# Shared-expert down products two chunks behind gate and up, with a third pair of operand buffers

## The chip, the cores and the metric

The kernel runs on one core of a Trainium2 chip. The metric is device time in microseconds, one launch, for the whole computation. Lower is better. The kernel before takes 1871.48 us, the median of 3 runs (1870.2 to 1871.99).

## The reference

A token stream of 2 x 2048 tokens with 256 features goes through three residual stages: half of a mixture-of-experts feed-forward, attention in groups of 64 tokens, and half of the same feed-forward again, each on a layer norm of the stream. Cut to what matters here:

```
x = x + 0.5 * ffn(layernorm(x))          # T = 4096 tokens, H = 256
x = x + attn(layernorm(x))               # 16 heads of 16, causal, groups of 64
x = x + 0.5 * ffn(layernorm(x))

ffn(x):  xn = rmsnorm(x);  probs = softmax(xn @ router_w.T);  top 2 of E = 8
         each expert takes its first 640 tokens:
           eout = (silu(xg @ rg[e]) * (xg @ ru[e])) @ rd[e]         # 256 -> 1024 -> 256
           routed += weight * eout
         shared = (silu(x @ sg) * (x @ su)) @ sd                    # 256 -> 2048 -> 256, all tokens
         return shared + routed
```

Everything is float32 at the interface.

## The kernel before

Every float32 operand of a large product is held as two float16 planes, a high and a low part. A product is then three float16 matmuls (high x high, high x low, low x high; the list TERMS).

The program has four phases. Phase a: layer norm and routing of 32 token tiles for the first feed-forward, beside the shared expert of 5 of the 8 token blocks (a block is 512 tokens). Phase b: the 8 experts of the first feed-forward. Phase c: the shared expert of the remaining 3 blocks, attention for 32 token tiles with layer norm and routing for the second feed-forward, and the shared expert of all 8 blocks of it. Phase d: the 8 experts of the second feed-forward.

The shared expert (`shared`) goes over the 2048 hidden features in 16 chunks of 128. For one chunk of one block, `gate_up` makes two groups of six matmuls of 512 columns (L306), the gate group and the up group, each into a tile "pgu" of PSUM; there are three such tiles in the pool `ps_gu`. Then the activation is made in the tile "sl" (float32): ScalarE applies Silu (L317, phase a) or Tanh (L313, phase c), in phase c VectorE completes it with L314, and VectorE multiplies in the up group (L319). ScalarE rounds the product to float16 into "hh" (L321), and VectorE writes the remainder into "hl" (L322). The pair hh and hl comes from the pool `hp` with two buffers; "sl" has two of its own.

The down products (`down`, L330) multiply hh and hl of a chunk with the chunk's rows of sd: twelve matmuls of 256 columns that add up over the 16 chunks in two PSUM tiles "po". After the last chunk VectorE adds the residual "xr" (L363, two instructions), and SP's queue stores the two halves of the block (L366). The tiles xr have two buffers in all, one block's worth, and are loaded by `res_load` (L344) ahead of chunk 2 of the block.

The down products of a chunk are not traced right after its gate and up products. `defer` holds one function back:

```
    def defer(self, f):
        p, self.pend = self.pend, f
        if p is not None:
            p()
```

So in the order of the source TensorE gets gate and up of chunk c, down of chunk c-1, gate and up of chunk c+1, and so on. The end of a phase calls `defer(None)` for the last one. The experts (`experts`, phases b and d) use the same `gate_up`, `down` and `defer`, with 640 tokens per expert in 8 chunks.

Beside the shared expert runs the work of the token tiles, written as generators: `tile1` (phase a) and `tile2` with `attn_tile` (phase c). `drive` takes one slot of this side work for every three steps of the shared expert, which is one slot per chunk. A tile of attention goes through the transposes L174, L533, L564 and L590 (DMAs on SP's queue), the projections L603 (tiles pqk, pv, pao), the scores L541 (psc), the products with the values L572 (py), and many small operations of VectorE, ScalarE and GpSimd; where it waits for a DMA it lets two slots pass. Its PSUM tiles come from the pool `ps_m` (three buffers in phases a and c).

The source gives a priority, not a fixed order: a planner with a timeline of its own orders the instructions of every engine, and an instruction whose operands are late in that timeline can be passed by later ones. [...]

Of the kernel before, what the change touches and what calls it, by code (L numbers as in the profile page):

```python
# [8 lines left out]
F32 = mybir.dt.float32  # L9
# [6 lines left out]
ALU = mybir.AluOpType  # L16
# [4 lines left out]
P = 128  # L21
H = 256
# [3 lines left out]
WS = 16.0  # L26
XP = UP * WS
NB = 8
BT = 512
# [8 lines left out]
class Net:  # L38
    def __init__(self, ctx, tc):
        self.tc = tc  # L40
        self.nc = nc = tc.nc
        pool = lambda name, bufs, **k: ctx.enter_context(tc.tile_pool(name=name, bufs=bufs, **k))
        self.cst = pool("cst", 1)
        self.wsh = pool("wsh", 1)
        self.tok = pool("tok", YB)
        self.xb = pool("xb", NB)
        self.xe = pool("xe", 2)
        self.sm = pool("sm", 2)
        self.dr = pool("dr", 1, space=DRAM)
        self.ps_gu = pool("ps_gu", 3, space=PSUM)  # L50
        self.pend = None
        self.anchor = None
        c = self.cst
        self.tri = c.tile([P, P], BF16, name="tri")
        nc.gpsimd.memset(self.tri, 1.0)
        nc.gpsimd.affine_select(
            out=self.tri, in_=self.tri, pattern=[[1, P]], compare_op=ALU.is_gt,
            fill=0.0, base=0, channel_multiplier=-1)
        self.ones = c.tile([P, P], BF16, name="ones")
        nc.gpsimd.memset(self.ones, 1.0)  # L60
        self.iota8 = c.tile([P, E], F32, name="iota8")
        for e in range(E):
            nc.gpsimd.memset(self.iota8[:, e:e + 1], float(e))
        self.mhalf = c.tile([P, 8], F32, name="mhalf")
        nc.gpsimd.memset(self.mhalf, -0.5)
        self.e1 = c.tile([P, 4], F32, name="e1")
        nc.gpsimd.memset(self.e1, 2.718281828459045)
        tk = self.sm.tile([P, 32], I32, name="tk", bufs=1)
        nc.gpsimd.iota(tk, pattern=[[P, 32]], base=0, channel_multiplier=1)
        self.tokid = c.tile([P, 32], F32, name="tokid")  # L70
        nc.vector.tensor_copy(self.tokid, tk)

    def phase(self, name, ntok, nout, nx=1, nsl=2):
        ctx = ExitStack()
        tc = self.tc
        pool = lambda n, bufs, **k: ctx.enter_context(
            tc.tile_pool(name=f"{name}_{n}", bufs=bufs, reuse_waits="tile", **k))
        self.ntok = ntok
        self.nsl = nsl
        self.hp = pool("hp", 2)  # L80
        self.xs = pool("xs", nx)
        self.raw = pool("raw", 2)
        self.at = pool("at", 1)
        self.ps_out = pool("po", nout, space=PSUM)
        self.ps_m = pool("pm", 5 - nout, space=PSUM)
        ctx.callback(lambda: self.defer(None))
        return ctx

    def m1(self, shape, dt, name):
        return self.ps_m.tile(shape, dt, name=name, tag="m")  # L90

    def defer(self, f):
        p, self.pend = self.pend, f
        if p is not None:
            p()

    def split(self, hi, lo, src):

# [249 lines left out]

    def shared(self, b, xb, src, dst, tanh=False, res=None):
        nc = self.nc  # L350
        outs = [self.ps_out.tile([P, BT], F32, name="po", tag="po") for _ in range(2)]
        for c in range(16):
            if c == 2 and res is None:
                res = self.res_load(src, b)
            h = self.hbuf()
            yield from self.gate_up(self.sgu[:, c], xb, h, tanh)

            def fin(c=c, h=h):
                self.down(outs, 4, h, self.sdw[:, :, c], c, 16)
                if c < 15:  # L360
                    return
                for i in range(2):
                    nc.vector.scalar_tensor_tensor(  # L363
                        out=res[i], in0=outs[i].rearrange("p (t f) -> p t f", f=H), scalar=0.5 / WS,
                        in1=res[i], op0=ALU.mult, op1=ALU.add)
                    nc.sync.dma_start(  # L366
                        out=dst[b * BT + i * 2 * P:b * BT + (i + 1) * 2 * P].rearrange("(t p) f -> p t f", p=P),
                        in_=res[i])

            self.defer(fin)  # L370
            yield
# [299 lines left out]
def run_slots(tiles, until):  # L671
    while not until():
        for _ in tiles.steps():
            pass


def drive(main, tiles, rate):

    credit = 0.0
    side = iter(())  # L680
    for _ in main:
        credit += 1.0
        for _ in range(2):
            if next(side, "end") == "end":
                break
        if credit >= rate:
            for _ in side:
                pass
            credit -= rate
            if not tiles.done():  # L690
                side = tiles.steps()
    for _ in side:
        pass


@with_exitstack
def macaron(ctx, tc, x, w_qkv, ln_w, w_proj, router_w, rg, ru, rd, sg, su, sd, out):
    nc = tc.nc
    x = x.rearrange("b s h -> (b s) h")
    out = out.rearrange("b s h -> (b s) h")  # L700
    n = Net(ctx, tc)
    R1 = n.route_init(0)
    R2 = n.route_init(1)
    R2["acc"] = out
    x2 = n.dr.tile([T, H], F32, name="x2")
    fbs = {}
    used = set()

    def new_fb(h, b):
        def get(t):  # L710
            if t == 0:
                assert h == 1 or (1, b) in used
                fb = fbs[(h, b)] = n.front_new()
                fb["pe"] = h == 1 and b < PEB
            return fbs[(h, b)]
        return get

    def tail(R, h, b, t):
        if t == 3:
            yield from n.route(R, b, fbs[(h, b)])  # L720

    def tile1(j):
        b, t = divmod(j, 4)
        y = n.load_tile(x, b, t)
        yield
        yield
        yield from n.front_steps(y, t, new_fb(1, b))
        yield from tail(R1, 1, b, t)

    def tile2(j):  # L730
        b, t = divmod(j, 4)
        yield from n.attn_tile(R1, j, x2, new_fb(2, b))
        yield from tail(R2, 2, b, t)

    def ready(h, b):
        return lambda: (h, b) in fbs and fbs[(h, b)]["n"] == 4

    def all_shared(key, b, src, dst, **k):
        yield from n.shared(b, fbs[key]["xb"], src, dst, **k)
        used.add(key)  # L740

    def fill(R):

        for e in range(E):
            z = n.raw.tile([P, 5, XW], F32, name="zero")
            nc.gpsimd.memset(z, 0.0)
            nc.vector.tensor_scalar_add(z[:, :, H], n.tokid[:, 0:5], float(T + e * CAP))
            nc.sync.dma_start(out=R["xg"][e * CAP:(e + 1) * CAP].rearrange("(t p) f -> p t f", p=P), in_=z)
            yield

    with n.phase("a", BT, 2, 10):
        n.ident = n.at.tile([P, P], F32, name="ident")
        make_identity(nc, n.ident)
        n.load_router(router_w)
        tiles = Tiles(tile1, 32, GAP_A)
        run_slots(tiles, ready(1, 0))
        n.load_shared(sg, su, sd)
        for _ in fill(R1):
            pass
        for b in range(NA):  # L760
            run_slots(tiles, ready(1, b))
            if b == 2:
                tiles.extra.append(fill(R2))
                for i in range(NA, NB):
                    nc.sync.dma_start(out=R1["acc"][i * BT:(i + 1) * BT], in_=x[i * BT:(i + 1) * BT])
            drive(all_shared((1, b), b, x, R1["acc"]), tiles, RATE_A)
        run_slots(tiles, tiles.done)
        cur = {}
        for _ in n.expert_load(R1, 0, cur):
            pass  # L770
    with n.phase("b", CAP, 3):
        n.experts(R1, rg, ru, rd, cur)
    with n.phase("c", BT, 2, 6, SLC):
        n.attn_init(w_qkv, ln_w, w_proj)
        tiles = Tiles(tile2, 32, GAP_C)
        for b in range(NA, NB):
            drive(all_shared((1, b), b, R1["acc"], R1["acc"], tanh=True), tiles, RATE_C)
        for b in range(8):
            run_slots(tiles, ready(2, b))
            drive(all_shared((2, b), b, x2, R2["acc"], tanh=True), tiles, RATE_C)  # L780
        run_slots(tiles, tiles.done)
        cur = {}
        for _ in n.expert_load(R2, 0, cur):
            pass
    with n.phase("d", CAP, 3):
        n.experts(R2, rg, ru, rd, cur)
# [10 lines left out]
SLC = 2  # L797
# [28 lines left out]
```

## Time and profile before

| | |
|---|---|
| median of 3 runs | 1871.48 us |
| the profiled execution's own time | 1875.79 us |
| its span, first to last instruction | 1874.1 us |
| mean granted TensorE clock | 0.994 |
| TensorE busy (matmuls) | 1786.8 us, 95% |
| VectorE busy | 1262.5 us, 67% |
| ScalarE busy | 942.1 us, 50% |
| GpSimd busy | 724.5 us, 39% |

Busy time counts the instructions of an engine as the profile draws them; matmuls are pipelined, so a drawn matmul is longer than the distance to the next one. PE stands for TensorE's matmuls, PEld for its weight loads, DVE for VectorE, ACT for ScalarE, POOL for GpSimd, SP for the queue that issues most DMAs. A row such as "L330 PE MATMUL po<-sdw,hl ... x1024 | busy, mean ns | idle" gives the line, the engine, what is written from what, the count, and the idle time of the engine just before such instructions with what ended it. In the view of waits a row is "engine line <- releaser: us in total, times, longest". By stage, phase a with the start takes about 0 to 340 us, phase b to about 690 us, phase c to about 1475 us, and phase d the rest; the phases overlap at their edges.

### The profile page before, as it was taken

To read this page: it belongs to the slowest core of one execution; us is meant where nothing else is said; L and a number is where in the kernel's file an instruction comes from. 1 tells how busy PE (TensorE), PEld (TensorE's weight loads), DVE (VectorE), ACT (ScalarE), POOL (GpSimd) and SP (SyncE) were. 2 spreads that over 40 slices of the span, in tenths; PEclk is the share of its full clock that TensorE was granted. 3 is DMA by queue.
4 is the path that set the end of the run, shared out by engine and by line. 5 is a ranking of instruction groups with operands and counts; after the bars stand their busy time and mean duration, and the time that the engine had idled before them with its cause. 6 is when DMAs were issued, how large, how long until landed. Compare 5 with 4: busy or idle time off the path is not lost.

```text
span 1874.1 us, 37396 instructions
## 1 busy us (share of the span) xinstructions
PE 1786.8 (95%) x13546; PEld 1191.7 (64%) x13546; DVE 1262.5 (67%) x3190; ACT 942.1 (50%) x1991; POOL 724.5 (39%) x943
## 2 busy tenths in 40 slices
PE   6899999999999999999999999999999999999996
PEld 3455555677777765666565655656566567777775
DVE  8756554456666656788888888888886556565663
ACT  5323323355555535666566666656643335555553
POOL 5743332011112223455757667575753001111122
PEclk9999999999999999999999999999999999999998
DMA  9742113045455424556657576766631304544542
GB/s 278 220 125 75 35 29 86 21 102 115 112 113 125 104 55 86 110 105 120 139 114 141 102 141 119 135 121 119 129 62 37 86 12 102 114 113 105 117 109 50
DMA packets 447481, 196.07 MB, mean 105 GB/s; under 512 B 302353, under 2 KB 444365, under 8 KB 447248
## 3 DMA queue, kind: packets, MB, share of 16 engines
q1 hardware_dynamic: 429632, 172.51, 41.1%
q0 software_dynamic: 17664, 21.17, 6.6%
q8 instruction: 106, 1.74, 0.4%
q14 instruction: 79, 0.65, 0.1%
HBM read 80.52 MB, written 52.33 MB: 71 GB/s over the span
## 4 chain that ended last, share of the span: by engine, by line
PE 57%; DVE 12%; POOL 10%; issue 9%; DMA 6%; ACT 4%; SPq 2%; POOLq 0%; DVEq 0%; ACTq 0%
PE pgu L306 36%; PE po L330 19%; POOL xg L287 3%; DVE hl L322 2%; DVE sl L319 2%; DVE sl L314 2%; DMA xg<-X,di 1%; DMA QT<-QK 1%; DMA rs<-in_L_ffn_su_dram 1%; POOL X L285 1%; DMA y<-in_L_attn_x_dram 1%; ACT hh L321 1%; POOL e L561 1%; DVE st L139 1%; POOL S L550 1%
## 5 line engine op out<-in xcount | busy, mean ns | idle before, releaser
L306 PE MATMUL pgu<-xb,sgu 128*128 128x512 f16 x3072 | 738.8, 380 | 26.3 <-DVE sl L319 11.1
L321 ACT CAST hh<-sl 128x512 f16<-128x512 f32 (+2 forms) x512 | 272.8, 533 | 563.3 <-DVE sl L319 521.4
L306 PE MATMUL pgu<-xe,wc 128*128 128x384 f16 (+1 forms) x3072 | 497.0, 299 | 0.5
L306 PEld LDWEIGHTS <-sgu 128*128 128x128 f16 x3072 | 293.2, 98 | 301.1 <-issue 35.8
L319 DVE SCALAR_TENSOR_TENSOR sl<-pgu,sl 128x512 f32<-128x512 f32 (+2 forms) x512 | 300.2, 587 | 204.7 <-PE pgu L306 171.4
L322 DVE TENSOR_TENSOR hl<-sl,hh 128x512 f16<-128x512 f32 (+2 forms) x512 | 328.4, 642 | 154.4 <-ACT hh L321 147.5
L330 PEld LDWEIGHTS <-hh 128*128 128x128 f16 x3328 | 320.6, 98 | 115.0 <-ACT hh L321 17.9
L306 PEld LDWEIGHTS <-wc 128*128 128x128 f16 x3072 | 300.5, 98 | 94.1 <-issue 1.8
L330 PE MATMUL po<-sdw,hh 128*128 128x256 f16 x2048 | 351.9, 273 | 7.3 <-ACT hh L321 6.9
L330 PE MATMUL po<-sdw,hl 128*128 128x256 f16 x1024 | 251.9, 274 | 15.8 <-DVE hl L322 10.8
L330 PE MATMUL po<-wd,hh 128*128 128x256 f16 x1280 | 223.4, 273 | 0.0
L330 PEld LDWEIGHTS <-hl 128*128 128x128 f16 x1664 | 162.9, 98 | 67.4 <-DVE hl L322 27.2
L317 ACT ACTIVATE sl<-pgu 128x384 f32<-128x384 f32 (+1 forms) x336 | 159.0, 473 | 55.3 <-PE pgu L306 34.2
L426 POOL DMA_INDIRECT out_dram<-eo,eid x40 | 64.6, 1616 | 313.8 <-DVE hl L322 248.3
L287 POOL DMA_INDIRECT xg<-X,di x128 | 136.0, 1063 | 112.2 <-DVE di L266 54.1
L426 POOL DMA_INDIRECT acc<-eo,eid x40 | 65.1, 1627 | 285.4 <-DVE hl L322 245.8
L330 PE MATMUL po<-wd,hl 128*128 128x256 f16 x640 | 152.4, 273 | 2.1 <-DVE hl L322 2.1
L314 DVE SCALAR_TENSOR_TENSOR sl<-sl,pgu 128x512 f32<-128x512 f32 x176 | 119.9, 681 | 38.3 <-ACT sl L313 37.2
L100 ACT ACTIVATE wc<-re 128x512 f16<-128x512 f32 x128 | 80.5, 629 | 83.3 <-PE pgu L306 52.9
L313 ACT ACTIVATE sl<-pgu 128x512 f32<-128x512 f32 x176 | 103.9, 591 | 33.3 <-PE pgu L306 31.8
L101 DVE SCALAR_TENSOR_TENSOR wc<-re,wc 128x512 f16<-128x512 f32 x128 | 88.3, 690 | 26.6 <-ACT wc L100 26.4
L550 POOL TENSOR_TENSOR S<-S,amx 128x1024 f32<-128x1024 f32 x32 | 63.7, 1990 | 81.3 <-DVE amx L549 74.4
(140 smaller groups left out, 1719.6 us busy)
## 6 DMA issues: line engine op xcount, KB each, us to landing
re<-in_L_ffn_rg_dram SPq DMA_DIRECT2D x128, 128.0 KB
re<-in_L_ffn_ru_dram SPq DMA_DIRECT2D x128, 128.0 KB
re<-in_L_ffn_rd_dram SPq DMA_DIRECT2D x128, 128.0 KB
xg<-zero SPq DMA_DIRECT2D x16, 650.0 KB
y<-acc SPq DMA_DIRECT2D x64, 128.0 KB
y<-in_L_attn_x_dram SPq DMA_DIRECT2D x32, 128.0 KB
acc<-xr SPq DMA_DIRECT2D x16, 256.0 KB
x<-y SPq DMA_DIRECT2D x32, 128.0 KB
```

Source lines behind the costliest of these rows:

```text
L101: nc.vector.scalar_tensor_tensor(out=lo, in0=src, scalar=WS, in1=hi, op0=ALU.mult, op1=ALU.subtract)
L287: i = nc.gpsimd.indirect_dma_start(out=R["xg"][:, :], out_offset=bass.IndirectOffsetOnAxis(ap=di[:, t, k:k + 1], axis=0), in_=X, in_offset ...
L306: nc.tensor.matmul(p, lhsT=wc[:, w, i, k, :], rhs=x[:, 2 * a + k, :], start=(j == 0), stop=(j == 5))
L313: nc.scalar.activation(s, p, AF.Tanh, scale=0.5 / XP)
L314: nc.vector.scalar_tensor_tensor(out=s, in0=s, scalar=1.0, in1=p, op0=ALU.add, op1=ALU.mult)
L317: nc.scalar.activation(s, p, AF.Silu, scale=1.0 / XP)
L319: nc.vector.scalar_tensor_tensor(out=s, in0=ps[1], scalar=1.0 / XP / (2.0 * XP if tanh else 1.0), in1=s, op0=ALU.mult, op1=ALU.mult)
L321: nc.scalar.copy(h[0], s)
L322: nc.vector.tensor_tensor(out=h[1], in0=s, in1=h[0], op=ALU.subtract)
L330: nc.tensor.matmul(o, lhsT=h[a][:, t * P:(t + 1) * P], rhs=wd[:, w], start=(c == 0 and j == 0 and t % 2 == 0), stop=(c == nch - 1 and j == 2),
L426: i = nc.gpsimd.indirect_dma_start(out=R["acc"][:, :], out_offset=bass.IndirectOffsetOnAxis(ap=ids[:, t:t + 1], axis=0), in_=eo, in_offset ...
L550: self.anchor = nc.gpsimd.tensor_tensor(out=S, in0=S, in1=mx.unsqueeze(2).to_broadcast([P, 16, 64]), op=ALU.subtract)
```

## The change

Wherever the shared expert runs (phases a and c), `defer` holds two functions back instead of one, so that the source order becomes gate and up of chunk c, down of chunk c-2, gate and up of chunk c+1, down of chunk c-1. The pool of hh and hl has three buffers there instead of two. The two PSUM tiles po of a block are now taken when its first down products are traced, not at the start of the block, and the function that is held back keeps its own reference to the block's xr tiles, since the next block's loop may have replaced the name by then. The end of a phase runs all that is still held back. The experts keep a distance of one chunk and two buffers.

```diff
-        self.pend = None
+        self.pend = []
+        self.lag = 1
...
-    def phase(self, name, ntok, nout, nx=1, nsl=2):
+    def phase(self, name, ntok, nout, nx=1, nsl=2, lag=1):
...
-        self.hp = pool("hp", 2)
+        self.hp = pool("hp", 1 + lag)
...
-        ctx.callback(lambda: self.defer(None))
+        self.lag = lag
+        ctx.callback(self.flush)
...
     def defer(self, f):
-        p, self.pend = self.pend, f
-        if p is not None:
-            p()
+
+        self.pend.append(f)
+        if len(self.pend) > self.lag:
+            self.pend.pop(0)()
+
+    def flush(self):
+        while self.pend:
+            self.pend.pop(0)()
...
     def shared(self, b, xb, src, dst, tanh=False, res=None):
         nc = self.nc
-        outs = [self.ps_out.tile([P, BT], F32, name="po", tag="po") for _ in range(2)]
+        outs = []
         for c in range(16):
             if c == 2 and res is None:
                 res = self.res_load(src, b)
             h = self.hbuf()
             yield from self.gate_up(self.sgu[:, c], xb, h, tanh)
-
-            def fin(c=c, h=h):
+            rs = res
+
+            def fin(c=c, h=h, rs=rs):
+                if c == 0:
+                    outs.extend(self.ps_out.tile([P, BT], F32, name="po", tag="po") for _ in range(2))
                 self.down(outs, 4, h, self.sdw[:, :, c], c, 16)
                 if c < 15:
                     return
                 for i in range(2):
                     nc.vector.scalar_tensor_tensor(
-                        out=res[i], in0=outs[i].rearrange("p (t f) -> p t f", f=H), scalar=0.5 / WS,
-                        in1=res[i], op0=ALU.mult, op1=ALU.add)
+                        out=rs[i], in0=outs[i].rearrange("p (t f) -> p t f", f=H), scalar=0.5 / WS,
+                        in1=rs[i], op0=ALU.mult, op1=ALU.add)
                     nc.sync.dma_start(
...
-                        in_=res[i])
+                        in_=rs[i])
...
-    with n.phase("a", BT, 2, 10):
+    with n.phase("a", BT, 2, 10, lag=2):
...
-    with n.phase("c", BT, 2, 6, SLC):
+    with n.phase("c", BT, 2, 6, SLC, lag=2):
```

## The prediction

> **What bounds the kernel now.** I read the page first (busy shares, slices), then the span cut into stages, then TensorE's waits by stage, then the timeline at the stalls. All durations come from the profiled execution: span 1874.1 us, own time 1875.79 us, which is 4.3 us above the 1871.48 us median of the runs; so I work out a difference and take it from the median.
>
> ```profile
> PE 1786.8 (95%) x13546; PEld 1191.7 (64%) x13546; DVE 1262.5 (67%) x3190; ACT 942.1 (50%) x1991; POOL 724.5 (39%) x943
> ...
> L306 PE MATMUL pgu<-xb,sgu 128*128 128x512 f16 x3072 | 738.8, 380 | 26.3 <-DVE sl L319 11.1 <-DVE sl L314 8.6 <-ACT sl L317 4.3
> ...
> L330 PE MATMUL po<-sdw,hh 128*128 128x256 f16 x2048 | 351.9, 273 | 7.3 <-ACT hh L321 6.9 <-issue 0.2
> ...
> L330 PE MATMUL po<-sdw,hl 128*128 128x256 f16 x1024 | 251.9, 274 | 15.8 <-DVE hl L322 10.8 <-issue 4.4
> ...
> L330 PE MATMUL po<-wd,hl 128*128 128x256 f16 x640 | 152.4, 273 | 2.1 <-DVE hl L322 2.1
> ```
>
> TensorE is the bound. Only its idle time can be won, and the rows name it: the shared expert's products wait about 23 us at the down products (7.3 + 15.8) and 26.3 us at gate and up. The experts' rows (wd) have almost none, so phases b and d offer nothing. By stage:
>
> ```profile
> 85.00:310.00 225.00, 214.91 (x1373) 127.28 (x1371) 121.62 (x437) 69.25 (x124) 91.05 (x171) 0.98 0.24 67
> ...
> 330.00:690.00 360.00, 357.29 (x2756) 269.34 (x2755) 210.17 (x443) 180.92 (x418) 65.69 (x46) 1.00 0.42 93
> ...
> 735.00:1426.00 691.00, 667.11 (x5505) 415.87 (x5506) 568.50 (x1425) 420.54 (x854) 421.05 (x522) 1.00 0.61 116
> ```
>
> The columns are window, length, then busy time of PE, PEld, DVE, ACT, POOL, then clock, DMA share, GB/s. In 735 to 1426 (attention beside shared chunks) VectorE is at 82% (568.5/691), so it is the next limit.
>
> A stall is under-read in these rows. Ten 256-column products in a row start 109 ns apart, yet each is drawn 273 ns long, so the first 164 ns of any gap look busy. The weight load in front, which is what carries the wait, shows it all. For 735 to 1426, first the load side, then the matmul side:
>
> ```profile
> PEld L330 <- DVE hl L322: 17.6, 31, 1.5
> ...
> PEld L330 <- DVE S L544: 4.2, 6, 0.7
> ...
> PE po L330 <- DVE hl L322: 8.2, 14, 1.2
> ...
> PE pgu L306 <- DVE sl L314: 7.1, 14, 0.9
> ...
> PE po L330 <- issue: 2.5, 6, 0.4
> ```
>
> Columns: total us, times, longest. True idle at the down products there: 8.2 + 2.5 = 10.7, plus 37 waiting loads (31 + 6) x 0.164 = 6.1, so 16.8 us. The same working on the other stages gives 12.0 us for 0 to 340 (8.2 us on the matmul rows, 23 waiting loads), 3.7 us for 690 to 735 (2.1 us, 10 loads) and 2.0 us for 1426 to 1475 (1.3 us, 4 loads). **Sum 34.5 us, 1.8% of the span.**
>
> What such a stall is made of:
>
> ```profile
> 1008.94 0.59 ACT L313 ACTIVATE sl<-pgu 128x512 f32<-128x512 f32 x1
> ...
> 1009.49 0.68 DVE L363 SCALAR_TENSOR_TENSOR xr<-po,xr 128x512 f32<-128x512 f32 x1
> ...
> 1009.74 0.38 PE L330 MATMUL po<-sdw,hh 128*128 128x256 f16 x2
> ...
> 1010.09 0.68 DVE L322 TENSOR_TENSOR hl<-sl,hh 128x512 f16<-128x512 f32 x1
> ...
> 1010.83 0.28 PE L330 MATMUL po<-sdw,hl 128*128 128x256 f16 x1 [0.71 <-DVE hl L322]
> ...
> 1011.93 1.46 PE L306 MATMUL pgu<-xb,sgu 128*128 128x512 f16 x6
> ```
>
> The down products are in TensorE's queue; hh is there, hl is late because VectorE did other work first (L363 here). TensorE stands, although the next gate group could run.
>
> **The change part by part.** *The order of the down products.* Work is equal: the same 12 down matmuls per chunk, 12 x 109 ns = 1.31 us, behind a gate and up of 12 x 216 ns = 2.59 us. What changes is age. From the end of a chunk's up group to its down products lie one down block and one gate-and-up, 1.31 + 2.59 = 3.9 us, against L319 0.68 + L321 0.62 + L322 0.68, about 2 us plus VectorE's backlog. With two chunks it is 7.8 us. The longest waits seen on weight loads at L330 are 3.4 us (hh) and 2.5 us (hl), under the 3.9 us added: every one of these stalls is covered. So up to -34.5 us.
>
> *What comes next.* Gate and up tiles have three PSUM buffers, unchanged: each group waits for the reader (L313/L314 or L319) of the group three before it. TensorE, no longer held, meets these sooner, and part of the gain returns there. With VectorE at 82% it is not full, and it has holes that move with TensorE (in 979.95 to 984.14 it is busy 1.55 of 4.19 us). I keep half in 690 to 735, 735 to 1426 and 1426 to 1475 (3.7 + 16.8 + 2.0 = 22.5, so 11.2 us), and three quarters of phase a's 12.0 (9.0 us), where VectorE is busy 121.62 of 225 us. Ends: none kept (0) and all kept (34.5).
>
> A rule speaks against keeping it. At the longest hl in this block the rows are
>
> ```profile
> 996.72 2.14 POOL L561 TENSOR_TENSOR e<-S,e 128x1024 f16<-128x1024 f32 x1
> ...
> 997.48 1.94 DVE L322 TENSOR_TENSOR hl<-sl,hh 128x512 f16<-128x512 f32 x1
> ...
> 999.48 0.28 PE L330 MATMUL po<-sdw,hl 128*128 128x256 f16 x1 [0.37 <-DVE hl L322]
> ...
> 999.68 0.68 DVE L314 SCALAR_TENSOR_TENSOR sl<-sl,pgu 128x512 f32<-128x512 f32 x1
> ```
>
> where hl takes 1.94 us for its usual 0.68. The Trainium skill, "SBUF — State Buffer", section "Who interferes with whom", says that a VectorE instruction with two SBUF inputs and a GpSimd one that reads SBUF exclude each other for the whole instruction. Then all of VectorE's queue is late, L314 and L319 with it; an extra buffer for hl cures nothing, the wait comes back at the gate and up groups, and the sum would be 0 for 735 to 1426: -12 us instead of -20. By the trace, L314 follows directly here and the next gate group waiting for it is 8 us later, so most is kept. I side with the row, but this is why I keep half, not all.
>
> *The third hh and hl.* 2 KB more per partition, no instruction: zero. hh of a chunk overwrites the one three back, whose down products stand a full gate-and-up earlier in TensorE's order, the same distance as with two buffers; sl keeps two. Without that cover ScalarE's L321 would wait for a down block, 1.31 us at most.
>
> *Outs taken at the first down products.* No instruction. Between a block's last down products and the next block's first there is still one gate-and-up (2.59 us), in which the two L363 (2 x 0.68) must run: zero, as now; ends 0 and 1 us at each of 14 seams.
>
> *The end of a block.* L363, two stores and their landing (2.63 us for the out<-xr at 1012.20 in the chain) come one chunk later, and the two loads of the next xr, in the same two buffers, follow at once instead of after a chunk. SP's queue can stand there. Now it waits 7.9 us in 5 of these places (SPq L344 <- DMA acc<-xr). Behind it in SP's queue are the attention transposes (L174, L533, L564, L590), on which TensorE's projections and scores wait. Cover: two slots, about 2 x 5.2 us (83.7 us per 16 chunks), lie between a transpose and its use, and TensorE now waits on a transpose once, 1.3 us. The load of xr itself has 13 chunks of time. I take zero; ends 0 and 14 seams x 1 us.
>
> *Flush.* Two down blocks end phases a and c; the first needs an hh and hl that are a chunk old and runs while the last ones are made: 0, ends -1.3 and +1.3 us for each phase.
>
> Sum: -9.0 - 11.2 = -20.2 us, so 1871.5 - 20.2 = **1851 us** (the profiled run's own 1875.8 would be 1855.6).
>
> **The rivals.** *A, the waits move to PSUM.* Gate and up wait 26.3 us already, with three buffers; VectorE or the chain gate, L313, L314, up is the true limit, and nearly everything returns. For it: 82% VectorE, the port rows. Against: the holes above, and phase a. Time: 4 us kept, 1867 us.
>
> *B, SP's queue at the seams (slower).* Store and reload back to back hold SP by 2 x 0.68 + 2.6 + issue, some 4.5 us, at 10 seams in phase c; attention transposes behind it come late, and TensorE, in order, stands at the projection (pqk, psc or py). It decides once the hold and a QT transpose pair (4.65 us in the chain) are over the two slots, 10.5 us; with the SP waits on TensorE (L590 <- PE pao, longest 9.6) that can be passed. Price: 3 us at 10 seams = +30, against -20: 1881 us. Against: SP's order is planned, other transfers can go first, and no such stall is in the trace now.
>
> *C, the order doesn't follow the source.* The instruction order is made by a planner from its own timeline: today down products already come split around gate groups (four hh, then gate matmuls, then hl). It may simply place work otherwise in VectorE's queue, with either sign: -4 to +12 us, 1875 us as its likeliest.
>
> **How the numbers follow.** Forecast 0.59 (all faster); A 0.17 (about 0.08 faster, 0.06 within, 0.03 slower); B 0.14 (slower); C 0.10 (0.02 faster, 0.03 within, 0.05 slower). The 0.2% bound, 3.7 us, is about what a measurement of this kernel can tell from no change. Faster 0.69, same 0.09, slower 0.22. The low end is everything kept, 1871.5 - 34.5 = 1837, a little lower for shorter half-clock stretches after stalls: 1836. The upper end takes in A, C and the lower part of B: 1877. That leaves out some 0.06 below and 0.13 above.
>
> **What would show it.** Right: weight loads at L330 waiting on L321 and L322 fall from some 50 us to under 10; 735 to 1426's work takes 8 or more us less; VectorE's share there rises by a point or more; the gate and up rows wait more than 26.3 us, but by less than 15 us more. A: that row rises by 25 us or so. B: TensorE waits on transposes (pqk or psc <- DMA) once a block, and SP's L344 rows on the store grow well over 7.9 us. C: VectorE's or TensorE's order of attention work differs between the traces. I am wrong if L330's waits are gone and the span is not at least 8 us shorter.

## The result: 0.25% slower, the waits gone and the time back at the phase edges

The changed kernel takes 1874.39 us (median of 12 runs) against 1869.87 us for the kernel before (12 runs beside it): ratio 1.0025, interval 1.0016 to 1.0034. The forecast was 1851 us, 20 us faster.

The page of the changed kernel first (lines move by seven to ten: L306 is now L313, L314 is L321, L319 is L326, L321 is L328, L322 is L329, L330 is L337, L400 is L410, L100 is L107).

```profile
PE 1785.6 (95%) x13546; PEld 1198.8 (64%) x13546; DVE 1265.9 (68%) x3190; ACT 943.3 (50%) x1991; POOL 723.1 (39%) x943
...
L313 PE MATMUL pgu<-xb,sgu 128*128 128x512 f16 x3072 | 735.4, 382 | 28.4 <-DVE sl L321 13.3
...
L313 PE MATMUL pgu<-xe,wc 128*128 128x384 f16 (+1 forms) x3072 | 502.7, 302 | 10.0 <-ACT wc L107 9.6
...
L337 PE MATMUL po<-sdw,hh 128*128 128x256 f16 x2048 | 360.5, 274 | 3.9 <-ACT hh L328 3.9
...
L337 PE MATMUL po<-sdw,hl 128*128 128x256 f16 x1024 | 278.9, 274 | 0.4 <-DVE hl L329 0.4
```

The wait that the change aims at has gone: 15.8 us became 0.4 at hl, 7.3 became 3.9 at hh. Gate and up hardly wait more (28.4 for 26.3). What is left at hh is one wait, at the start of phase c. A row that waited 0.5 us before now waits 10.0: the experts' products, for a weight (wc) that ScalarE makes. Before, it was

```profile
L306 PE MATMUL pgu<-xe,wc 128*128 128x384 f16 (+1 forms) x3072 | 497.0, 299 | 0.5
```

By stage, with the columns as before:

```profile
85.00:310.00 225.00, 219.19 (x1420) 131.70 (x1418) 124.15 (x450) 70.61 (x126) 93.29 (x172) 0.98 0.28 73
330.00:690.00 360.00, 347.69 (x2679) 262.42 (x2677) 205.11 (x436) 176.87 (x414) 69.37 (x53) 0.99 0.45 99
...
357.00:364.00 7.00, 6.75 (x28) 3.89 (x29) 2.88 (x6) 2.99 (x8) 0.00 (x0) 0.55 0.54 147
735.00:1426.00 691.00, 667.05 (x5540) 422.26 (x5539) 574.88 (x1428) 423.97 (x860) 419.64 (x526) 1.00 0.60 116
```

Phase a does more in the same time (1420 matmuls instead of 1373). Phase c does 0.6% more (5540 for 5505) with the same idle time. The stretch 330 to 690, where nothing was to be changed, loses: PE is busy 347.69 us instead of 357.29. In 357 to 364 the granted clock is 0.55.

Starts of the same product in the two traces show where time was won and lost:

| TensorE starts | before | after | difference |
|---|---|---|---|
| 80th shared chunk (last of phase a) | 357.6 | 345.7 | -11.8 us |
| second expert of phase b | 401.6 | 397.7 | -3.9 us |
| 97th shared chunk | 758.0 | 755.4 | -2.6 us |
| 241st shared chunk (phase c) | 1475.2 | 1469.1 | -6.1 us |
| second expert of phase d | 1577.8 | 1579.2 | +1.4 us |

Phase a wins 11.8 us, and the edge to the experts takes 7.9 back. At the 97th chunk the changed kernel has one down block fewer behind it (94 for 95), 1.3 us of work; so the start of phase c costs 2.6 us, and the stretch from there to the 241st chunk wins 4.8. The second edge takes 7.5. The two profiled executions are 1875.79 and 1876.0 us, so the profiled one of before is longer than any of the 12 runs of its kernel (1867.28 to 1874.34); the 4.5 us between the medians are not seen whole in this pair of traces.

What happens at an edge (timeline of the changed kernel):

```profile
349.99 0.69 DVE L329 TENSOR_TENSOR hl<-sl,hh 128x512 f16<-128x512 f32 x1 [0.69 <-ACT hh L328]
...
350.70 0.37 SPq L410 DMA_DIRECT2D re<-in_L_ffn_rg_dram  x1
...
352.16 0.27 PE L337 MATMUL po<-sdw,hl 128*128 128x256 f16 x1
...
353.77 0.50 SPq L410 DMA_DIRECT2D re<-in_L_ffn_ru_dram  x1
...
356.57 0.63 ACT L107 ACTIVATE wc<-re 128x512 f16<-128x512 f32 x1 [6.61 <-DMA re<-in_L_ffn_rd_dram]
...
357.25 1.14 PE L313 MATMUL pgu<-xe,wc 128*128 128x384 f16 x3 [4.82 <-ACT wc L107]
```

The last hl of phase a ends, 20 ns later SP issues the first load of expert weights, the weights land and are split, and TensorE has stood for 4.8 us after its last down product. The kernel before issued that load at 313.8 us:

```profile
313.83 0.37 SPq L400 DMA_DIRECT2D re<-in_L_ffn_rg_dram  x1
```

In the changed kernel SP's queue names what held it, in 300 to 355 us and in 1440 to 1540 us:

```profile
SPq L410 <- DVE hl L329: 40.1, 1, 40.1
```

```profile
SPq L410 <- DVE hl L329: 51.9, 1, 51.9
```

A weight load has no operand in common with hl; so it should be the memory that it waits for. From the sizes in the source, per partition: phase a's pool of sl, hh and hl has 2 x 2 KB + 2 x 2 KB = 8192 bytes with two buffers, 10240 with three. The experts' pool, with 640 tokens and two buffers, has 2 x 2 KB + 2 x 2.5 KB = 9216. The experts' weight tiles come next in memory, at 9216: behind phase a's sl, hh and hl before the change, on top of their last kilobyte after it. The experiments below test this.

In phase c the waits have moved (735 to 1426, matmul side), first the scores and value products before, then the rows after:

```profile
PE py L572 <- DVE S L544: 3.3, 6, 0.5
PE py L572 <- DVE qk L511: 2.1, 6, 0.7
PE psc L541 <- DVE S L544: 0.8, 4, 0.2
```

```profile
PE psc L551 <- DVE S L554: 9.8, 6, 1.6
PE py L582 <- DVE qk L521: 6.2, 6, 1.1
PE pgu L313 <- DVE sl L321: 5.8, 12, 0.6
PE psc L551 <- DVE vs L516: 1.9, 6, 0.3
```

The down products' 10.7 us are gone; the attention's scores and value products (psc, py), which waited 6.2 us, wait 17.9.

### The profile page after: what moved, and what is told of

It is laid out like the page before. It is cut to its first block, busy times and chain, and to the rows that moved or that the text cites. A ratio compares the mean times of both kernels' runs of the same rounds, so it can differ in the third digit from the quotient of the medians.

```text
span 1874.3 us, 37378 instructions
## 1 busy us (share of the span) xinstructions
PE 1785.6 (95%) x13546; PEld 1198.8 (64%) x13546; DVE 1265.9 (68%) x3190; ACT 943.3 (50%) x1991; POOL 723.1 (39%) x943
## 4 chain that ended last, share of the span: by engine, by line
PE 57%; DVE 14%; POOL 9%; issue 4%; DMA 3%; ACT 2%; SPq 1%; POOLq 0%; DVEq 0%; ACTq 0%
PE pgu L313 37%; PE po L337 18%; POOL xg L294 3%; DVE hl L329 2%; DVE sl L326 2%; DVE sl L321 2%; DVE amx L559 1%; DVE Y L588 1%; POOL ss L511 1%; DVE qk L521 1%; POOL X L292 1%; ACT hh L328 1%; DMA acc<-eo,eid 1%; POOL e L571 1%; DVE st L146 1%
## 5 line engine op out<-in xcount | busy, mean ns | idle before, releaser
L313 PE MATMUL pgu<-xb,sgu 128*128 128x512 f16 x3072 | 735.4, 382 | 28.4 <-DVE sl L321 13.3
L328 ACT CAST hh<-sl 128x512 f16<-128x512 f32 (+2 forms) x512 | 273.0, 533 | 511.2 <-DVE sl L326 510.8
L313 PE MATMUL pgu<-xe,wc 128*128 128x384 f16 (+1 forms) x3072 | 502.7, 302 | 10.0 <-ACT wc L107 9.6
L313 PEld LDWEIGHTS <-sgu 128*128 128x128 f16 x3072 | 296.6, 98 | 315.0 <-issue 41.5
L329 DVE TENSOR_TENSOR hl<-sl,hh 128x512 f16<-128x512 f32 (+2 forms) x512 | 326.6, 638 | 163.9 <-ACT hh L328 162.3
L326 DVE SCALAR_TENSOR_TENSOR sl<-pgu,sl 128x512 f32<-128x512 f32 (+2 forms) x512 | 301.2, 588 | 192.6 <-PE pgu L313 175.2
L337 PEld LDWEIGHTS <-hh 128*128 128x128 f16 x3328 | 322.1, 98 | 112.5 <-ACT hh L328 4.4
L313 PEld LDWEIGHTS <-wc 128*128 128x128 f16 x3072 | 302.1, 98 | 107.1 <-ACT wc L107 10.1
L337 PE MATMUL po<-sdw,hh 128*128 128x256 f16 x2048 | 360.5, 274 | 3.9 <-ACT hh L328 3.9
L337 PE MATMUL po<-sdw,hl 128*128 128x256 f16 x1024 | 278.9, 274 | 0.4 <-DVE hl L329 0.4
L337 PE MATMUL po<-wd,hh 128*128 128x256 f16 x1280 | 224.1, 273 | 0.0
L337 PEld LDWEIGHTS <-hl 128*128 128x128 f16 x1664 | 162.9, 98 | 33.1 <-DVE hl L329 3.1
L337 PE MATMUL po<-wd,hl 128*128 128x256 f16 x640 | 152.5, 273 | 1.2 <-DVE hl L329 1.1
L321 DVE SCALAR_TENSOR_TENSOR sl<-sl,pgu 128x512 f32<-128x512 f32 x176 | 119.6, 680 | 33.1 <-ACT sl L320 32.6
L107 ACT ACTIVATE wc<-re 128x512 f16<-128x512 f32 x128 | 80.4, 628 | 80.8 <-PE pgu L313 52.3
L564 ACT COPY V<-vs 64x512 f16<-64x512 f16 x128 | 78.8, 616 | 13.6 <-PE py L582 11.3
```

Source lines behind the costliest of these rows:

```text
L107: nc.scalar.mul(hi, src, WS)
L313: nc.tensor.matmul(p, lhsT=wc[:, w, i, k, :], rhs=x[:, 2 * a + k, :], start=(j == 0), stop=(j == 5))
L321: nc.vector.scalar_tensor_tensor(out=s, in0=s, scalar=1.0, in1=p, op0=ALU.add, op1=ALU.mult)
L326: nc.vector.scalar_tensor_tensor(out=s, in0=ps[1], scalar=1.0 / XP / (2.0 * XP if tanh else 1.0), in1=s, op0=ALU.mult, op1=ALU.mult)
L328: nc.scalar.copy(h[0], s)
L329: nc.vector.tensor_tensor(out=h[1], in0=s, in1=h[0], op=ALU.subtract)
```

## The experiments

All ratios are to the kernel before, measured beside each run; microseconds worked out from them take 1870 us as the whole. "A block" is 16 chunks of phase c with attention, the mean of the 10th to the 13th block in the profile.

**Edges and layout.** The first four kernels ran on one chip.

e1_pad, the changed kernel with the experts' pool made as long as the shared one's:

```diff
-        self.hp = pool("hp", 1 + lag)
+        self.hp = pool("hp", 3)
```

> The changed kernel with three hh and hl buffers in the expert phases too, which still use them at a distance of one; only the place of what lies behind them in SBUF moves. Theory E (edges): in the changed kernel the experts' weight tiles share addresses with the third buffers of the phase before, so their first loads wait for its last hl (SP waits 40.1 and 51.9 us), and TensorE stands 5.0 and 4.9 us and then runs some 3 us more slowly. Then both stalls go, the first re loads come before 320 us again, and the time is 14 to 16 us under the changed kernel: 1858 to 1860, ratio to before 0.993 to 0.995. Theory F (flush): the edges stall because two down blocks are left over at the end and come last in TensorE's queue; then nothing changes, 1873 to 1876.

Measured 0.9968 (0.9955 to 0.9981): 6.0 us under before, and 0.0057 under the changed kernel's ratio, 10.7 us. SP's queue again issues the weights early:

```profile
309.06 0.37 SPq L410 DMA_DIRECT2D re<-in_L_ffn_rg_dram  x1
309.48 0.46 SPq L410 DMA_DIRECT2D re<-in_L_ffn_ru_dram  x1
```

The view of waits lists none of TensorE any more in 340 to 380 and in 1480 to 1570 us. The edges are explained as theory E has it; by the runs the size is 10.7 us (some 3 either way, from the two intervals) for the expected 14 to 16. In the two traces the way from phase a's last chunk to the second expert takes 44.1 us for 52.0, and from the 241st chunk to the second expert of phase d 103.5 for 110.0: 14.5 us together. Phase a's last chunk starts at 353.6 in this profile, not 345.7. Theory F is out, since the two left-over down blocks are still there.

e2_third_only, the kernel before with

```diff
-        self.hp = pool("hp", 2)
+        self.hp = pool("hp", 3 if ntok == BT else 2)
```

> The kernel before (distance one) with a third hh and hl buffer in phases a and c alone. Theory E: the third buffer brings the two edge stalls without any of the gain, +12 to +16 us: 1882 to 1886, SP waiting some 40 us at L400 on an hl. Theory F: without the longer distance nothing is left over, 1867 to 1873, no change.

Measured 1.0092 (1.0072 to 1.0112), 17 us slower without any longer distance. The first edge, by SP's and by TensorE's waits:

```profile
SPq L400 <- DVE hl L322: 45.7, 2, 41.7
```

```profile
PE pgu L306 <- ACT wc L100: 4.9, 1, 4.9
```

The second edge is the same: SP waits 53.8 us for an hl, TensorE 5.0 us for a weight. The third buffer alone makes the stalls.

e3_layout, the same with three buffers in all four phases (`pool("hp", 3)` in the kernel before):

> The kernel before (distance one) with three buffers in all phases: the control for layout. Theory E: no edge stall and no longer distance, so no change, 1866 to 1874. Theory F: the same. If it is faster by 5 us or more, e1's gain would be partly the layout's and not the distance's.

Measured 1.0007 (0.9999 to 1.0015): no change. Against it, e2 shows the edges' price with nothing else different: 1.0092 - 1.0007 = 0.0085, 16 us for two edges. The traces agree: 52.4 us for 44.1 at the first edge, 109.9 for 102.6 at the second, 15.6 us. And e1 against it shows the distance alone: 0.9968 - 1.0007 = -0.0039, 7.3 us.

e4_a_only, e1_pad with `n.phase("c", BT, 2, 6, SLC)`, so that phase c keeps a distance of one:

> As e1, but the distance of two in phase a alone; phase c at one. By the profiles phase a gained 11.8 us up to its last chunk and phase c about 4 us more. Theory E: 10 to 12 us under the kernel before, 1858 to 1860, within 4 us of e1. Theory G (the waits merely move within phase a, and the gain there is the profiled run's own luck): 1866 to 1871.

Measured 0.9978 (0.9969 to 0.9986), 4.1 us under before: within 4 us of e1_pad, as theory E says, but not the 10 to 12 us; the time alone lies in theory G's range. Luck is not all of it, though: against e3_layout 0.9978 - 1.0007 = -0.0029, 5.4 us. The profiles of phase a vary. With a distance of two its last chunk starts between 345.7 and 359.2 us over the runs of this study, with one between 355.6 and 360.3; the means are 351.7 (seven profiles) and 358.2 (six). The profile of the changed kernel was the fortunate end.

h1_c_only, the complement (`n.phase("a", BT, 2, 10)` in e1_pad):

> The complement of e4_a_only: three buffers in all phases, the distance of two in phase c alone. If the two phases' gains add up, it is e3_layout's 1.0007 less the difference of e1_pad and e4_a_only (0.0010): 0.9997, between 0.998 and 1.001, and a block of phase c takes 83.2 to 83.3 us against 83.7. If phase c keeps half of its 16.8 us of waits at the down products, as was forecast (8 us), it is 0.996 or less.

Measured 1.0007 (0.9999 to 1.0015), equal to e3_layout, though a block of 16 chunks in phase c takes 83.27 us by the profile (e3_layout 83.63). The gain of phase c is 0 by the runs, give or take 2 us, and about 4 us by the profile's blocks.

**What takes the gain in phase c.**

f1_halfmax, e1_pad with less VectorE work per attention tile (a softmax doesn't depend on the value that is subtracted, as long as nothing overflows):

```diff
-        nc.vector.tensor_reduce(out=mx, in_=S, axis=AX.X, op=ALU.max)
+        nc.vector.tensor_reduce(out=mx, in_=S[:, :, 0:32], axis=AX.X, op=ALU.max)
```

> e1_pad with the softmax maximum (L549 of the kernel before, 1.21 us of VectorE per attention tile) taken over the first 32 keys alone: VectorE has 0.6 us less per tile, 19 us in all, in the stretch where the attention waits pile up. Theory V (in phase c VectorE's queue is the limit, so with two chunks' distance the waits only change their place in it): a block of phase c, 83.2 us in e1_pad, loses 1.2 us or more, and the time falls 12 us or more under e1_pad's ratio of 0.9968, to 0.990. Theory B (what is short is the three PSUM buffers of the attention products, held through a chain over ScalarE and GpSimd): less than 0.4 us a block, ratio 0.994 to 0.997.

Measured 0.9954 (0.9938 to 0.9971). A block takes 82.52 us, 0.73 less than e1_pad, for four tiles with 2.4 us of VectorE less. The ratio is in theory B's range and not told apart from e1_pad's 0.9968; the block is between the theories. psc still waits, 11.5 us for 9.9.

f4_halfmax_one, the same edit in e3_layout:

> e3_layout (distance one) with the maximum over 32 keys. Theory V: VectorE's queue makes the hl late at distance one as well, so the gain is the same 12 us or more, ratio 0.993 or less. Theory B: 0.997 to 1.001.

Measured 1.0011 (1.0004 to 1.0018), a block 83.61 us: nothing. Theory V is out at a distance of one: VectorE's sum of work isn't the limit there.

f2_bank4, e1_pad with a fourth PSUM buffer for the attention:

```diff
-                    outs.extend(self.ps_out.tile([P, BT], F32, name="po", tag="po") for _ in range(2))
+                    outs.extend(self.ps_out.tile([P, BT], F32, name="po", tag="po") for _ in range(self.nout))
+                    outs.extend(outs[:2 - self.nout])
...
-    with n.phase("c", BT, 2, 6, SLC, lag=2):
+    with n.phase("c", BT, 1, 6, SLC, lag=2):
```

> e1_pad with a fourth PSUM buffer for the attention products in phase c. To free it, both halves of a block's down products add up in one tile there (so the two halves of the block are mixed; the work of every engine is the same). Theory B: the waits of the scores and of the products with the values (psc, py; 18 us of phase c on the matmul rows of e1_pad) fall under 6 us and a block takes 82 us or less; ratio 0.988 to 0.991. Theory V: the waits return at gate and up or elsewhere, a block stays at 83 us, ratio 0.996 to 0.998.

This kernel, f3 and g2 leave out keeping the two halves of a block apart. Measured 0.9929 (0.9912 to 0.9945), a block 81.85 us. TensorE's waits in 755 to 1420 us (in f2 and f3 the lines stand one or two further on):

```profile
PE pgu L314 <- DVE sl L322: 14.7, 6, 2.6
PE py L584 <- DMA ET<-e: 0.6, 1, 0.6
PE po L338 <- issue: 0.2, 1, 0.2
```

The waits of psc and py are gone, as theory B says, and the ratio misses its range by 0.002: one wait of some 2.5 us per block has appeared at gate and up (14.7 us for 5.8). The wait at the attention's three PSUM buffers was what took the place of hl.

f3_bank4_one, the same in e3_layout:

> e3_layout (distance one) with the same fourth buffer and the same mixed halves in phase c. If the short buffers are what takes the gain of the longer distance, then at distance one they matter less: the psc and py waits are only 7 us there, the hl waits stay, and a block falls from 83.7 us by 0.3 us at most; ratio 0.998 to 1.001. Theory V: no change, 1.000.

Measured 0.9931 (0.9914 to 0.9947), a block 81.60 us; expected was hardly any gain. The waits now:

```profile
PE po L331 <- DVE hl L323: 10.8, 11, 1.4
PE pgu L307 <- DVE sl L315: 3.1, 3, 1.1
PE po L331 <- ACT hh L322: 1.6, 3, 0.6
PE py L574 <- issue: 1.5, 3, 0.6
```

So the edit is worth 0.0076 of the time at a distance of one too, without looking like it: the small psc and py rows fall, and yet the hl waits stay. In e3_layout the rows were

```profile
PE py L572 <- DVE S L544: 3.3, 6, 0.5
PE py L572 <- DVE qk L511: 2.2, 6, 0.7
PE psc L541 <- DVE S L544: 1.0, 5, 0.2
```

6.5 us together. The edit has two parts, the fourth buffer and the mixed halves, and no run has the second alone; the down matmuls start 109 ns apart (median) with and without it. With four buffers the longer distance is worth nothing in time (0.9929 and 0.9931): the buffers' shortage decides where the wait goes, but its end does not bring the lost gain back.

g1_gu2, a fourth attention buffer taken from gate and up instead:

```diff
-        self.ps_gu = pool("ps_gu", 3, space=PSUM)
...
+        self.ps_gu = pool("gu", ngu, space=PSUM)
         self.ps_out = pool("po", nout, space=PSUM)
-        self.ps_m = pool("pm", 5 - nout, space=PSUM)
+        self.ps_m = pool("pm", 8 - ngu - nout, space=PSUM)
...
-    with n.phase("c", BT, 2, 6, SLC, lag=2):
+    with n.phase("c", BT, 2, 6, SLC, lag=2, ngu=2):
```

> e1_pad with PSUM cut differently in phase c: two buffers for gate and up instead of three, four for the attention products instead of three; nothing is left out. At a distance of two, down products are always ready to fill the time between two groups, so two gate and up buffers might do. Theory B (the attention's buffers are short, gate and up have room): psc and py waits gone, ratio 0.990 to 0.994, under e1_pad's 0.9968. Theory L (VectorE's lateness is what counts, and it only picks which buffer runs out): the wait goes to gate and up, L306's waits in phase c rise from 6 us to 25 us or more, ratio 0.998 to 1.010.

Measured 1.0127 (1.0109 to 1.0145), slower than even theory L's range. Gate and up wait 19.4 us for L321 (expected 25 or more), and hl and the transposes come back:

```profile
PE pgu L313 <- DVE sl L321: 19.4, 19, 3.5
PE py L582 <- DMA ET<-e: 7.3, 8, 2.9
PE po L337 <- DVE hl L329: 7.0, 8, 2.3
```

Gate and up have no PSUM buffer to spare.

g2_bank4_half, f2_bank4 with the shorter maximum:

> f2_bank4 (distance two, a fourth buffer for the attention products, halves mixed) with the maximum over 32 keys as well. Theory L: with the buffers' shortage gone VectorE's 0.6 us a tile count: the one wait left in a block, 2.6 us for L314 at gate and up, gets shorter by a microsecond or more, the half-clock stretch behind it goes (granted clock 1.00 instead of 0.98 in a block), and a block takes 80.5 us or less instead of 81.85; ratio 0.986 to 0.989. Theory B: nothing further to gain, 81.5 to 82 us a block, ratio 0.992 to 0.994.

Measured 0.9925 (0.9909 to 0.9942), a block 81.91 us, as theory B says. The one wait per block is a little shorter (0.6 us, not a microsecond), and the block's clock stays low:

```profile
PE pgu L314 <- DVE sl L322: 11.0, 6, 2.0
```

```profile
1010.00:1091.50 81.50, 79.73 (x666) 50.44 (x665) 66.49 (x182) 53.08 (x108) 54.96 (x71) 0.98 0.69 131
```

What the shorter wait saves the clock takes, by an estimate: the waits are 3.7 us shorter in all, but five of the six are followed by a stretch of half clock, three of six in f2, and two more stretches cost 3.4 us (the last section has the rows). VectorE works 66.5 of 81.5 us there and still makes the wait. In f2 it works from 1083.8 to 1089.0 us without a gap, most of it for the attention, before its L322 ends and TensorE goes on. That the bunching of its work counts and not the sum is a reading that fits both runs; it was not tested.

Of the kernels that keep the halves apart, e4_a_only (0.9978), e1_pad (0.9968) and f1_halfmax (0.9954) beat both the kernel before and the changed one.

## Why the prediction was wrong

In the prediction's own sum two terms failed: "the third hh and hl: zero", and the gain that is kept, -20.2 us. With -7.3 us for the gain and +10.7 to +16 us for the buffers the sum is +3.4 to +8.7 us; the medians are 4.5 us apart. Its own sign of being wrong has come: the waits at the down products are gone, and the span is not 8 us shorter.

**The third hh and hl: the step that failed.** The prediction put them at "no instruction: zero", with L321's reuse as the only thing to lose. They cost 10.7 us (e1_pad against the changed kernel) to 16 us (e2 against e3). The step looked at what the buffer does inside its phase; it did not ask what stands at those addresses in the next phase. Not all of it is the stall itself: after 4.7 to 5.0 us without a matmul the granted clock is 0.55 (357 to 364 us) and 0.62 over 7 us:

```profile
1539.00:1546.00 7.00, 6.95 (x32) 4.06 (x33) 3.71 (x8) 4.67 (x9) 0.00 (x0) 0.62 0.49 140
```

By an estimate from these two rows that adds about 3 us at each edge.

**The order of the down products: right.** Every kernel with the longer distance in phase c, but g1_gu2, has next to no wait at the down products there, and in the changed kernel the weight loads at L337 wait 8.6 us in all, under the 10 that the prediction gave as a sign.

**What is kept: mis-sized.** Kept were to be 9.0 us in phase a and 11.2 us in the rest. By the runs the distance gives 7.3 us in all (e1 against e3), 5.4 of it in phase a (e4 against e3), and none that timing shows in phase c (h1). The prediction looked for the next wait at gate and up; in the changed kernel those hardly rose. The next in line were the attention's own PSUM buffers, which it named nowhere. This is the wait of each block at the scores:

```profile
999.93 1.14 DVE L329 TENSOR_TENSOR hl<-sl,hh 128x512 f16<-128x512 f32 x1 [1.18 <-ACT hh L328]
1000.48 1.11 POOL L172 TENSOR_TENSOR X<-z,X 128x256 f16<-128x256 f32 x1
1000.99 0.63 DVE L509 TENSOR_SCALAR ss<-ss 128x2 f32<-128x2 f32 x1
1001.53 0.68 DVE L554 TENSOR_TENSOR S<-psc,mask 128x512 f32<-128x512 f32 x1
1002.26 0.39 PE L551 MATMUL psc<-QT 128*128 128x64 f16 x8 [1.62 <-DVE S L554]
```

The second half of the scores needs a buffer; VectorE frees one with L554, and comes to it late, behind an hl for which it has itself waited 1.18 us. TensorE no longer stands at hl here, but VectorE does, and the scores behind it pay: the wait was passed on, not removed.

**The rule on the shared port**, which the prediction weighed and set aside, would have put phase c's share at 0, which is what was measured. Its place was wrong (psc and py, not gate and up), its reason is there in part: in all six blocks hl takes 1.13 us for its usual 0.68 and L509 0.63 for 0.16, both beside GpSimd's L172. That is some 0.9 of the 1.6 us, by an estimate from these rows. No run moves L172 away, so what it costs in time is not shown.

**Rival A**, the waits move to PSUM, had the right idea at the wrong buffers, and with a fourth attention buffer (f2) at the right ones: there the wait stands at gate and up. **Rival B** did not happen: SP's waits for the stores at L351 did grow, to 18.9 us in 22 places (before 10.7 in 9, of which the prediction counted one row), but TensorE waits for a transpose once in 735 to 1426, 0.3 us. **Rival C**, another order, doesn't explain it: in the block around 960 to 1005 us the scores stand behind the same numbers of gate and up matmuls in both traces (1644, 1692, 1728, 1740), though they are not always split alike among the down matmuls.

**The outs, the end of a block, the flush**, each put at zero: VectorE's wait at L373 fell from 6.4 to 2.5 us, and the longer waits of SP at L351 have no wait of TensorE behind them. Whether one of them costs under 1 us was not tried.

**Open:** why phase a's gain varies so much from run to run (its last chunk between 345.7 and 359.2 us); why in phase c neither the fourth buffer nor less work for VectorE brings the gain back; the start of phase c, where a cast of attention weights on ScalarE waits 10.0 us and TensorE 3.9 us behind it in the changed kernel (e2 has the 10.0 too, yet from the second expert to the 97th chunk takes 358.9 us, e3 358.6); and the 4 us that the pair of traces does not show.

## What to carry to other kernels

When one phase's pool grows, compare its end with the pools of the phase that follows at the same addresses: a buffer that costs no instruction can hold the next phase's first loads until the last use of the old tile. A wait that stops an engine (here TensorE at hl, with other matmuls ready behind it) is worth its length only if nothing behind it is short as well; before counting it as gain, list every pool that the work behind it needs, and ask whether the engine it waited for is any earlier. Waits counted in a profile don't say which shortage is the costly one: in e3_layout 6.5 us of waits at psc and py stood beside an edit worth 0.76%, while taking some 12 us of hl and hh waits away with that edit in place (f2 for f3) brought nothing.

## What was not expected of the hardware

A stall can be followed by a slow stretch. Behind 4.8 us without a matmul the granted clock was 0.55 over 7 us. Shorter waits did it too, but not each time. Two waits of f2 at gate and up, and the clock behind each:

```profile
926.61 1.46 PE L314 MATMUL pgu<-xb,sgu 128*128 128x512 f16 x6 [2.62 <-DVE sl L322]
926.60:930.60 4.00, 3.99 (x41) 2.67 (x41) 3.15 (x4) 2.46 (x4) 2.62 (x2) 1.00 0.46 74
1089.02 2.72 PE L314 MATMUL pgu<-xb,sgu 128*128 128x512 f16 x6 [2.58 <-DVE sl L322]
1089.00:1092.00 3.00, 2.98 (x21) 1.32 (x21) 2.23 (x2) 1.45 (x3) 2.64 (x2) 0.50 0.29 48
```

Half clock for 3.4 us followed three of f2's six waits (1.9 to 2.6 us) and five of g2's six (1.2 to 2.0 us), and the block's mean is 0.98 in both; in the kernel before it is 0.74 in 105 to 108 us, behind a wait of 2.0. Waits of up to 1.6 us in the changed kernel's phase c and of up to 1.4 us in f3_bank4_one left the clock at 1.00; a block of f3:

```profile
1010.00:1091.85 81.85, 79.24 (x666) 49.84 (x664) 69.47 (x178) 53.52 (x110) 57.11 (x71) 1.00 0.69 129
```

So the length of the wait alone doesn't decide here. Such a stretch costs 1.7 us by an estimate (3.4 us at half clock). The Trainium skill, "TensorE: Matmul & The Clock Gate", section "What's actually happening", has half clock after an idle window of about 3.4 us; by that these waits would cost no more than themselves. Here less was enough, so the measurement decides. So one long wait can be dearer than several short ones of the same sum.
